# Adjacency masks kept in DRAM as pairs of tiles, and a 14th tile moved per block in the last attention

## The chip, the cores and the metric

The kernel runs on one core of a Trainium2 chip. The metric is the device time of one launch in microseconds (us). A kernel is profiled in one more execution on the chip, and the times quoted from the profile belong to that execution.

## The reference, cut to what matters

The inputs are node features `x` (4096 x 512) and a 0/1 adjacency matrix `adj` (4096 x 4096). Two graph layers with residuals follow each other. All arithmetic is in float32.

```python
# layer 0: adj serves as both patterns, so there is one attention, used twice
h = relu(layernorm(x))
Xw = einsum("hnd,hde->hne", heads(h), W)              # 4 heads of 128
sig = sigmoid(f1[:, :, None] + f2[:, None, :])        # f1, f2: two scores per node and head
att = masked_softmax(adj * sig, adj != 0)
Xn = batchnorm(concat(einsum("hij,hjd->hid", att, Xw)))
emb = batchnorm(elu(Xn @ Wm.T + bm) + Xn)
Y = einsum("hij,hjd->hid", att, heads(emb))           # the same attention again
Y = elu(concat(einsum("hnd,hed->hne", Y, W)))
x = x + batchnorm(elu(Y @ Wd.T + bd) + Y)
# layer 1: another attention over the same adjacency
h = relu(layernorm(x))
feats = einsum("nf,hfo->hno", h, W1)
logits = leaky_relu(e_s[:, :, None] + e_n[:, None, :], 0.2) - 1e10 * (1 - adj)
x = x + relu(concat(einsum("hnm,hmo->hno", softmax(logits), feats) + b))
```

## The kernel before, in words

**Stages.** They follow each other: a front end (layer norm, projection of the nodes, scores); the first attention, called enc; a dense block; the second attention, dec; a second dense block; the values of layer 1; the third attention, gat. `attention` (from L222) is one function that is used three times.

**Blocks and steps.** An attention has eight blocks, one for each of four heads and two halves of the target nodes (2048 of them, `TB`). A block has 32 steps `j`, one for each group of 128 source nodes. In a step, ScalarE computes a tile `e` of 128 x 2048 unnormalized weights (L471 and L472 in enc and dec, L922 in gat), VectorE multiplies it by the mask tile `a` of that step (L473 or L923), and TensorE multiplies it into four PSUM banks (L377). Tiles `e` come from a ring of 8 in enc and 9 in gat (`ebufs` and `EP`).

**Denominators.** Every tile `e` must also be summed over the source nodes. There are three ways to do that. VectorE adds the tile to `acc` (L400 for the first two tiles, L402 after that). TensorE multiplies it by ones (`add_to_den`, L266). Or GpSimd issues two accumulating DMAs, one for each half of the tile, which add it to another tile, `into` (L392). Which steps go where is written in the constants `ENC...` and `GAT...`: the first tuple holds the steps that are moved by DMA, the second those that go to TensorE by ones, and VectorE takes the rest. A third element that is true puts the reading of `into` by TensorE off to step 1 of the next block. In gat `into` is the tile `w` (from block 1 on), and the first move of a block overwrites it. The moves of one half follow each other, since each adds to what the one before it wrote.

**Masks.** The adjacency matrix arrives as float32 and transposed (`adjT`). `copy_adjacency` has GpSimd issue eight DMAs (L502), one after each of the last seven parts of the front end and one more at the end. Each reads 1024 rows by 2048 columns of float32 and writes them as bytes to one DRAM tile of `masks`, of 1024 x 2048, whose rows 128 q to 128 q + 127 are the mask of one step. I call them the casts. The first four hold the masks of the first half of the targets. They are held back until half of `x` is loaded (`half_loaded`).

**Loads.** The SyncE queue loads the mask of each step (L211), 128 rows of 2 KB, to one of five tiles. The load for step `j + 5` waits until VectorE is done with step `j`. The first five are issued in the front end, behind the load of the score row `row0` (L204). The queue also carries the loads of `x` before that (L496). In dec, every fifth step reads the finished tile that enc stored in `ekeep`, and needs no mask. In enc those stores go out on ScalarE's queue in the first two blocks (L362) and on SyncE's later.

**After a block.** The denominators of a block are inverted in the course of the next: they go out to DRAM (L273), come back as columns (L278), are inverted on VectorE (L282, L283), and are spread (L286, L291). GpSimd's queue carries these small DMAs in enc, the same queue as the casts and the accumulating moves; ScalarE's carries them in gat.

Of the kernel before, what the change touches and what calls it, by code (L numbers as in the profile page):

```python
# [31 lines left out]
FP = mybir.dt.float32  # L32
U8 = mybir.dt.uint8
# [6 lines left out]
N, F, H, D, P = 4096, 512, 4, 128, 128  # L40
IB = 512
NIB = N // IB
NJ = N // P
C = IB // P

TB = 2048
NTB = N // TB
SB = TB // IB

MG = 8  # L50
# [13 lines left out]
ENC = (0, 2, 5, 7, 10, 12, 15, 17, 20, 22, 25), (8, 9, 30, 31)  # L64

GAT_FIRST = (0, 2, 4, 6, 8, 10, 12, 14, 16, 18, 20, 22, 24), (30, 31)
GAT = tuple(range(3, 28, 2)), (31,), True

GAT_LAST = (3, 5, 7, 9, 11, 13, 15, 17, 19, 21, 23), (30, 31)

# [15 lines left out]
def kernel(ctx, tc, x, xT, adjT, w0, w0T, v0, wencT, wdecT, vecs, w1, w1T, a1, outT):  # L86
    nc = tc.nc
    consts = ctx.enter_context(tc.tile_pool(name="consts", bufs=1))
# [43 lines left out]


    score = consts.tile([P, 2, NTB, H, NJ // NTB], FP, name="score")
    jcol = consts.tile([P, NTB, H, NJ // NTB], FP, name="jcol")
    jcol2 = consts.tile([P, NTB, H, NJ // NTB], FP, name="jcol2")
    nq = consts.tile([P, NTB, H, NJ // NTB], FP, name="nq")

    def column(t, j, h):
        j = j % (NJ // NTB), j // (NJ // NTB)  # L140
# [20 lines left out]
    ekeep = [[[dram.tile([P, TB], FP, name=f"ekeep{h}_{t}_{k}") for k in range(NJ // KEEP)] for t in range(NTB)]  # L161
             for h in range(H)]

    masks = [[dram.tile([MG * P, TB], U8, name=f"mask{t}_{g}") for g in range(NJ // MG)] for t in range(NTB)]

    def everywhere(d, row, lo, n):

# [36 lines left out]
        return nc.sync.dma_start(rowb, everywhere(d, row, 0, TB))  # L204

    def mask_tile(keep):
        return keep.tile([P, TB], U8, name="a", bufs=5)

    def load_mask(a, tb, j):

        return nc.sync.dma_start(a, masks[tb][j // MG][(j % MG) * P:(j % MG + 1) * P, :])  # L211

    @contextmanager
    def pinned(behind):
# [7 lines left out]
    def attention(what, keep, pools, weights, values, row_of, out, finish, ebufs, modes=None, invert=None,  # L222
# [25 lines left out]
        spool, made, masks0 = pools, 0, list(masks0)  # L248
# [76 lines left out]
        for n, (h, tb) in enumerate(blocks):  # L325
# [4 lines left out]
            into = sums2[0 if n else 1] if moved else None  # L330

            po, ahead, late = [bank() for _ in range(SB - 1)], [], []
            adds, held, stores, at_end, next_row = [], [], [], [], None
            for j in range(NJ):

                with pinned(products_of):
                    for f in later.pop(j, []):
                        f()
                with pinned([a_load, *products_of, last_main] if j else []):
                    if (n, j) in extras:  # L340
                        extras[n, j](a_load)
                    if not last and j == NJ - 10:
                        next_row = next_row_of(*blocks[n + 1])
                e = weight_tile()
                store = j % KEEP == KEEP - 1 and kept is not None
                if store and kept == "read":
                    a_load = nc.sync.dma_start(e, ekeep[h][tb][j // KEEP])
                else:
                    if masks0:
                        a, a_load = masks0.pop(0)  # L350
                    else:
                        a = mask_tile(keep)
                        a_load = load_mask(a, tb, j)

                    with pinned([*(products_of[:1] if kept == "read" and n == 0 and j < 8 else ()),
                                 *(behind if n == 0 and j < EP else ())]):
                        products_of = weights(e, rowb, a, j, h, SB if NJ * n + j < in_parts0 else 1)


                    if stores and (store if n > 1 else j % KEEP == KEEP - 3):  # L360
                        k, t = stores.pop()
                        (nc.sync if n > 1 else nc.scalar).dma_start(ekeep[h][tb][k], t)  # L362
                    if store:
                        stores.append((j // KEEP, e))

                def products():
                    nonlocal last_main, last_ones

                    with tc.issue_after(last_ones.ins) if last_ones is not None else nullcontext():

                        if j == EVICT:
                            po.append(bank())
                            for k, t in ahead:
                                nc.tensor.matmul(po[-1], block(values[h], k), t[:, (SB - 1) * IB:SB * IB],  # L374
                                                 start=(k == 0), stop=False)
                        for s, b in enumerate(po):
                            last_main = nc.tensor.matmul(b, block(values[h], j), e[:, s * IB:(s + 1) * IB],  # L377
                                                         start=(j == 0), stop=(j == NJ - 1))
                    last_ones = None


                if last and invert is not None and j >= NJ - (1 if kept is not None else 4):
                    late.append((j, e))
                else:
                    products()
                if j < EVICT:
                    ahead.append((j, e))
                if invert is not None:
                    if j in moved:

                        for into_half, e_half in in_parts(2, into, e):
                            nc.gpsimd.dma_start(into_half, e_half, **({"accum_op": ALU.add} if j > moved[0] else {}))  # L392
                    elif j in by_ones:
                        held.append(e)
                    else:
                        adds.append(e)
                        if last and kept is not None and j >= NJ - 6:
                            at_end.append(e)
                        elif len(adds) == 2:
                            nc.vector.tensor_add(acc, *adds)  # L400
                        elif len(adds) > 2:
                            nc.vector.tensor_add(acc, acc, e)  # L402

                    if j == NJ - 1:
                        for t in at_end:
                            nc.vector.tensor_add(acc, acc, t)

                    if held and j + 1 not in by_ones:
                        with tc.issue_after(last_main.ins):
                            for t in held:  # L410
                                add_to_den(den, t, not begun)
                                begun = True
                        held = []
                    if j == NJ - 1:
                        with tc.issue_after(last_ones.ins) if last_ones is not None else nullcontext():
                            if moved and not ends_later:
                                add_to_den(den, into, not begun)
                                begun = True
                            add_to_den(den, acc, not begun, not ends_later)
# [58 lines left out]
    with tc.tile_pool(name="keep", bufs=1) as keep:  # L478

        with tc.tile_pool(name="f_small", bufs=1) as small, tc.tile_pool(name="f_work", bufs=2) as work:  # L480
# [18 lines left out]
            def copy_adjacency(n, behind):  # L499

                t, g = divmod(n, NJ // MG)
                cast = nc.gpsimd.dma_start(masks[t][g], adjT[g * MG * P:(g + 1) * MG * P, t * TB:(t + 1) * TB])  # L502
                tc.add_manual_dep(cast.ins, behind.ins.name,
                                  mybir.DependencyInfo(mybir.DependencyClass.Sync, mybir.DependencyReason.DATA),
                                  reason="others first")

            for ib in range(NIB):
# [59 lines left out]
                if ib == SB - 1:  # L567
                    store_rows(rows[0], targets(0))
                    row0 = keep.tile([P, TB], FP, name="rowb", bufs=2)
                    row0_load = load_row(row0, rows[0], 0)  # L570
                    with tc.issue_after(row0_load.ins):
                        masks0 = []
                        for j in range(5):
                            a = mask_tile(keep)
                            masks0.append((a, load_mask(a, 0, j)))
            store_rows(rows[1], targets(1))
# [148 lines left out]
    v1 = xd  # L725

    edge = ctx.enter_context(tc.tile_pool(name="edge", bufs=1))
    with tc.tile_pool(name="l_small", bufs=1) as small, tc.tile_pool(name="l_work", bufs=2) as work:
        x1 = [R[2]] + [small.tile([P, N], FP, name=f"x1_{o}") for o in range(1, C)]

# [215 lines left out]
    with tc.tile_pool(name="gat", bufs=1) as spool:  # L946
# [10 lines left out]

        with tc.issue_after(last_pe.ins):
            attention("gat", spool, spool, gat_weights, v1, lambda h, tb: (rowsg, tb * H + h), out_gat,
                      (scaled_gat, add_to_output), 7, lambda n: (GAT_FIRST, *[GAT] * (H * NTB - 2), GAT_LAST)[n],  # L960
                      (N * TINY, ALU.add), sums=R[2][:, 0:TB], sums2=(row0, R[2][:, TB:N]), row0=row0, in_parts0=3,
                      extras={(0, 1): rest_of_rows, (H * NTB - 1, NJ - 10): load_last, (H * NTB - 1, NJ - 4): add_bias},
                      finish_last=finish_gat)


def _inputs(x, adj, w):
# [5 lines left out]
    return {  # L972
        "x": x,
        "xT": x.T,
        "adjT": adj.T,
        "w0": w["L0_gnn_W"].transpose(1, 0, 2),
        "w0T": w["L0_gnn_W"].transpose(2, 0, 1),
        "v0": w["L0_gnn_V"][..., 0].transpose(2, 0, 1),
# [27 lines left out]
```

## Time and profile before

| what | before |
|---|---|
| median of 3 runs | 3241.08 us (3240.25 to 3242.4) |
| the profiled execution, its time | 3242.24 us |
| its span from first to last instruction | 3240.5 us |
| TensorE matmul, busy | 3187.6 us (98%) |
| VectorE, busy | 2665.8 us (82%) |
| ScalarE, busy | 2581.8 us (80%) |
| bytes moved by DMA | 580.60 MB |
| enc, dec and gat, roughly | 62 to 1040, 1200 to 2065 and 2315 to 3240 us |

Time on the chip around the span is 1.7 us. Matmuls are pipelined, so a busy TensorE isn't TensorE at its peak, and busy shares are averages over stages that have different limits.

### The profile page before, as it was taken

Reading aid. Unit: us, or ns where it says so; the run is one execution under the profiler, and the core shown is the slowest. Engines: PE = TensorE matmul, PEld = TensorE weight load, DVE = VectorE, ACT = ScalarE, POOL = GpSimd, SP = SyncE. Lnnn points to the kernel's source line nnn. Section 1 sums busy time; section 2 is a strip of 40 time slices with the busy share of each in tenths; the row PEclk is TensorE's granted clock in tenths of the full one; section 3 lists DMA queues with packets and bytes.
Section 4 is the critical chain, followed back from the end, with each engine's and each line's share of the span. In section 5 each row is a group of like instructions: output and inputs, shape, how many; then the busy total and the mean of one; then the engine's idle time right before and its main releaser. Section 6 shows DMA issues by size and latency. Waiting matters only on the chain.

```text
span 3240.5 us, 25992 instructions
## 1 busy us (share of the span) xinstructions
PE 3187.6 (98%) x8675; PEld 1477.3 (46%) x8675; DVE 2665.8 (82%) x1945; ACT 2581.8 (80%) x1825; POOL 477.6 (15%) x624
## 2 busy tenths in 40 slices
PE   7999999999999999999999999999999999999998
PEld 6334444444444464444444444448644444444443
DVE  7989999999999665655665665585699999999998
ACT  7999999999997459999999999566765665665663
POOL 3001211211210000000000000025412222122221
PEclk9999999999999999999999999999999999999999
DMA  9998988988986024443443443231489999899996
GB/s 210 198 198 242 273 223 231 268 222 229 268 236 159 7 69 141 143 143 126 139 153 130 133 145 133 62 123 63 130 201 221 214 229 237 218 213 235 229 215 156
DMA packets 212023, 580.60 MB, mean 179 GB/s; under 512 B 25168, under 2 KB 28272, under 8 KB 195888
## 3 DMA queue, kind: packets, MB, share of 16 engines
q0 software_dynamic: 68256, 223.56, 36.5%
q1 hardware_dynamic: 132200, 332.53, 30.1%
q10 hardware_dynamic: 11432, 22.85, 2.0%
q8 instruction: 68, 1.11, 0.1%
q14 instruction: 67, 0.55, 0.0%
HBM read 378.15 MB, written 84.30 MB: 143 GB/s over the span
## 4 chain that ended last, share of the span: by engine, by line
PE 50%; DVE 24%; issue 13%; DMA 9%; ACT 3%; DVEq 0%; POOL 0%; SPq 0%; ACTq 0%; POOLq 0%
PE ps L377 35%; DVE e L923 7%; DVE R L402 7%; PE ps L639 7%; DVE e L473 4%; DMA a<-mask 4%; DMA w<-e 4%; DVE acc L402 4%; PE ps L828 3%; DMA acc<-e 2%; ACT e L471 1%; PE den L266 1%; ACT e L472 1%; PE ps L699 1%; PE ps L374 1%
## 5 line engine op out<-in xcount | busy, mean ns | idle before, releaser
L377 PE MATMUL ps<-e,R 128*128 128x512 f32 x6008 | 2608.1, 595 | 25.0 <-DVE e L473 20.6
L377 PEld LDWEIGHTS ps<-e,R 128*128 128x128 f32 x6008 | 1137.8, 190 | 1489.6 <-issue 1394.3
L473 DVE TENSOR_TENSOR e<-e,a 128x2048 f32<-128x2048 f32 (+1 forms) x470 | 1053.2, 2261 | 388.1 <-ACT e L472 365.0
L471 ACT ACTIVATE e<-rowb,score 128x2048 f32<-128x2048 f32 (+1 forms) x470 | 911.8, 1968 | 78.7 <-PE ps L377 43.4
L472 ACT ACTIVATE e<-e 128x2048 f32<-128x2048 f32 (+1 forms) x470 | 869.3, 1879 | 7.9 <-DVE e L473 2.6
L922 ACT ACTIVATE e<-rowb,nq,jcol 128x2048 f32<-128x2048 f32 x224 | 459.4, 2088 | 265.6 <-DMA w<-e 141.2
L923 DVE SCALAR_TENSOR_TENSOR e<-e,jcol,a 128x2048 f32<-128x2048 f32 (+1 forms) x265 | 591.2, 2260 | 2.8 <-ACT e L922 2.8
L402 DVE TENSOR_TENSOR R<-R,e 128x2048 f32<-128x2048 f32 x128 | 291.1, 2274 | 0.0
L402 DVE TENSOR_TENSOR acc<-acc,e 128x2048 f32<-128x2048 f32 x121 | 276.4, 2285 | 0.9
L392 POOL DMA_DIRECT2D w<-e x178 | 149.4, 845 | 610.8 <-DMA w<-e 294.6
L639 PE MATMUL ps<-R,w 128*128 128x512 f32 x512 | 220.3, 592 | 0.6 <-DVE w L597 0.6
L392 POOL DMA_DIRECT2D acc<-e x146 | 122.5, 888 | 521.0 <-DMA acc<-e 233.4
L291 POOL DMA_DIRECT2D rb<-rinvs x60 | 33.9, 569 | 1054.8 <-DVE R L587 867.2
L639 PEld LDWEIGHTS ps<-R,w 128*128 128x128 f32 x512 | 97.2, 190 | 122.7 <-issue 117.7
L828 PE MATMUL ps<-w1x,hT 128*128 128x260 f32 x512 | 115.5, 384 | 1.4 <-ACT hT L806 1.4
L828 PEld LDWEIGHTS ps<-w1x,hT 128*128 128x128 f32 x512 | 96.5, 190 | 19.8 <-issue 3.3
L922 ACT ACTIVATE e<-w,nq,jcol 128x2048 f32<-128x2048 f32 (+1 forms) x41 | 67.4, 1708 | 25.5 <-DMA R<-e 25.4
L865 POOL TENSOR_TENSOR vacc<-vacc,R 128x128 f32<-128x128 f32 x120 | 65.8, 577 | 45.3 <-ACT R L858 44.9
L662 DVE SCALAR_TENSOR_TENSOR ex<-ex,re 128x512 f32<-128x512 f32 x64 | 44.9, 702 | 32.8 <-ACT re L661 32.6
L660 ACT ACTIVATE ex<-ps,bias 128x512 f32<-128x512 f32 x32 | 22.0, 689 | 58.8 <-PE ps L639 56.4
L858 ACT ACTIVATE R<-ps,rstd 128x128 f32<-128x128 f32 x128 | 38.5, 371 | 29.3 <-PE ps L828 25.6
L266 PE MATMUL den<-e,ones 128*32 128x512 f32 x416 | 51.7, 608 | 3.9 <-DVE e L923 3.9
(175 smaller groups left out, 1255.9 us busy)
## 6 DMA issues: line engine op xcount, KB each, us to landing
a<-mask SPq DMA_DIRECT2D x720, 256.0 KB, 4.1
w<-e POOLq DMA_DIRECT2D x178, 512.0 KB, 6.9
acc<-e POOLq DMA_DIRECT2D x146, 512.0 KB, 6.9
e<-ekeep SPq DMA_DIRECT2D x48, 1024.0 KB, 4.9
ekeep<-e SPq DMA_DIRECT2D x36, 1024.0 KB, 6.9
mask<-in_adjT POOLq DMA_DIRECT2D x8, 2048.0 KB, 105.4
rowb<-rows SPq DMA_DIRECT2D x16, 1024.0 KB, 5.9
rb<-rinvs POOLq DMA_DIRECT2D x60, 256.0 KB, 4.6
```

Of the source, the lines that this page charges most:

```text
L266: last_ones = nc.tensor.matmul(den[s * 32:(s + 1) * 32, :], ones[:, 0:32], t[:, s * IB:(s + 1) * IB], start=start, stop=stop)
L377: last_main = nc.tensor.matmul(b, block(values[h], j), e[:, s * IB:(s + 1) * IB], start=(j == 0), stop=(j == NJ - 1))
L392: nc.gpsimd.dma_start(into_half, e_half, **({"accum_op": ALU.add} if j > moved[0] else {}))
L402: nc.vector.tensor_add(acc, acc, e)
L471: nc.scalar.activation(e, rowb, AF.Tanh, bias=column(score[:, 1], j, h), scale=0.5)
L472: last_act = nc.scalar.activation(e, e, AF.Exp, scale=0.5)
L473: last_dve = nc.vector.tensor_mul(e, e, a)
L639: last = nc.tensor.matmul(z, w[:, fb, o * P:(o + 1) * P], nodes(src[fb], ib), start=(fb == 0), stop=(fb == C - 1))
L828: m = nc.tensor.matmul(banks[k][:, 0:2 * DX], hT[:, fb, c * P:(c + 1) * P], w1x[:, fb, 2 * k:2 * k + 2, :].rearrange("p h x -> p (h x)"), ...
L865: nc.gpsimd.tensor_add(vacc[:, h, :], vacc[:, h, :], block(v1[h], j))
L922: last_act = nc.scalar.activation(e, rowb, AF.Relu, bias=column(nq, j, h), scale=column(jcol, j, h))
L923: last_dve = nc.vector.scalar_tensor_tensor(e, e, column(jcol2, j, h), a, ALU.add, ALU.mult)
```

## The change

**Masks in pairs.** The host orders the adjacency matrix by half of the targets, then by pair of steps, then by the 128 rows, and puts the 2048 columns of the two steps of a pair side by side in a row of 4096. A cast now reads 512 such rows, which follow each other without a gap in DRAM, and writes 512 rows of 4096 bytes, which fill a DRAM tile without a gap as well. The number of casts, their bytes and their place in the program stay. A mask tile holds two steps, there are three of them instead of five, and one DMA of 128 rows of 4 KB loads both steps. The front end loads three pairs ahead. In dec a pair is loaded whole even where one of its steps reads `ekeep`.

**Room.** Three small tiles (`jcol`, `jcol2`, `nq`, 512 bytes a partition each) are taken out of the pool that lives from the start and put into one that is opened after dec.

**Moves in gat.** In blocks 1 to 6 the tiles of 14 steps (3, 5, ..., 29) are moved by DMA instead of 13 (3, 5, ..., 27). In blocks 1, 3 and 5 step 31 still goes to TensorE, so the extra tile is taken from VectorE. In blocks 2, 4 and 6 step 31 goes to VectorE, so in effect the extra tile is taken from TensorE. Blocks 0 and 7 stay.

```diff
-GAT = tuple(range(3, 28, 2)), (31,), True
+GAT = tuple(range(3, 30, 2)), (31,), True
+GAT_EVEN = tuple(range(3, 30, 2)), (), True
...
-    masks = [[dram.tile([MG * P, TB], U8, name=f"mask{t}_{g}") for g in range(NJ // MG)] for t in range(NTB)]
+    masks = [[dram.tile([MG // 2 * P, 2 * TB], U8, name=f"mask{t}_{g}") for g in range(NJ // MG)] for t in range(NTB)]
...
-        return keep.tile([P, TB], U8, name="a", bufs=5)
+        return keep.tile([P, 2, TB], U8, name="a", bufs=3)
...
-        return nc.sync.dma_start(a, masks[tb][j // MG][(j % MG) * P:(j % MG + 1) * P, :])
+        q = j % MG // 2
+        return nc.sync.dma_start(a.rearrange("p k i -> p (k i)"), masks[tb][j // MG][q * P:(q + 1) * P, :])
...
-                    if masks0:
-                        a, a_load = masks0.pop(0)
-                    else:
-                        a = mask_tile(keep)
-                        a_load = load_mask(a, tb, j)
+                    if two_masks is None or j // 2 != two_masks[1]:
+                        if masks0:
+                            both, a_load = masks0.pop(0)
+                        else:
+                            both = mask_tile(keep)
+                            a_load = load_mask(both, tb, j)
+                        two_masks = both, j // 2
+                    a = two_masks[0][:, j % 2, :]
...
-                cast = nc.gpsimd.dma_start(masks[t][g], adjT[g * MG * P:(g + 1) * MG * P, t * TB:(t + 1) * TB])
+                cast = nc.gpsimd.dma_start(masks[t][g], adjT[n * MG // 2 * P:(n + 1) * MG // 2 * P, :])
...
-                        for j in range(5):
+                        for j in range(0, 6, 2):
...
-                      (scaled_gat, add_to_output), 7, lambda n: (GAT_FIRST, *[GAT] * (H * NTB - 2), GAT_LAST)[n],
+                      (scaled_gat, add_to_output), 7, lambda n: (GAT_FIRST, *[GAT, GAT_EVEN] * (H * NTB // 2 - 1), GAT_LAST)[n],
...
-        "adjT": adj.T,
+        "adjT": adj.T.reshape(NJ // 2, 2, P, NTB, TB).transpose(3, 0, 2, 1, 4).reshape(N // 2 * NTB, 2 * TB),
```

More of the change, by code (lines that the diff above doesn't have):

```diff
@@ L134 @@
     score = consts.tile([P, 2, NTB, H, NJ // NTB], FP, name="score")
-    jcol = consts.tile([P, NTB, H, NJ // NTB], FP, name="jcol")
-    jcol2 = consts.tile([P, NTB, H, NJ // NTB], FP, name="jcol2")
-    nq = consts.tile([P, NTB, H, NJ // NTB], FP, name="nq")
     def column(t, j, h):
@@ L332, in attention @@
             po, ahead, late = [bank() for _ in range(SB - 1)], [], []
-            adds, held, stores, at_end, next_row = [], [], [], [], None
+            adds, held, stores, at_end, next_row, two_masks = [], [], [], [], None, None
             for j in range(NJ):
@@ L727 @@
     edge = ctx.enter_context(tc.tile_pool(name="edge", bufs=1))
+    jcol = edge.tile([P, NTB, H, NJ // NTB], FP, name="jcol")
+    jcol2 = edge.tile([P, NTB, H, NJ // NTB], FP, name="jcol2")
+    nq = edge.tile([P, NTB, H, NJ // NTB], FP, name="nq")
     with tc.tile_pool(name="l_small", bufs=1) as small, tc.tile_pool(name="l_work", bufs=2) as work:
```

## The prediction

> **What bounds the kernel now.** I read the windows by stage first. Columns: the stretch and its length, then busy time (and instructions) of PE, PEld, DVE, ACT and POOL, then TensorE's clock, the DMA share and GB/s.
>
> ```profile
> 160.00:200.00 40.00, 37.03 (x115) 14.48 (x113) 35.73 (x18) 38.88 (x22) 0.00 (x0) 1.00 1.05 194
> 600.00:640.00 40.00, 40.00 (x97) 17.78 (x94) 38.70 (x22) 40.00 (x22) 7.51 (x10) 1.00 1.05 276
> 2680.00:2720.00 40.00, 40.00 (x95) 17.76 (x94) 40.00 (x23) 23.48 (x13) 7.72 (x9) 1.00 1.04 245
> ```
>
> In enc's later blocks (second line) ScalarE never stops: 32 x (1.89 + 1.80) = 118.2 us a block, 3.695 us a step. The DMA engines are full from the front end on. In gat (third line) TensorE and VectorE are both never idle, so I looked at which of them sets the end, in the timeline of PE:
>
> ```profile
> 3213.03 1.06 PE L266 MATMUL den<-e,ones 128*32 128x512 f32 x8 [2.33 <-DVE e L923]
> 3217.49 1.93 PE L266 MATMUL den<-e,ones 128*32 128x512 f32 x8 [1.61 <-DVE e L923]
> ```
>
> TensorE waits there 2.33 + 1.61 = 3.94 us for VectorE, so VectorE's sum ends gat, with TensorE 3.94 us behind it.
>
> Then the masks. The waits of VectorE between 100 and 200 us and between 200 and 320 us (total, times, longest):
>
> ```profile
> DVE e L473 <- DMA a<-mask: 7.2, 6, 3.1
> ...
> DVE e L473 <- DMA a<-mask: 5.0, 4, 2.7
> ```
>
> The DMA queues between 24 and 34 us, and between 100 and 200 us (packets, MB, share of 16 engines; q0 is GpSimd's, q1 SyncE's, q10 ScalarE's):
>
> ```profile
> q0 software_dynamic: 434, 0.89, 87.5%
> q1 hardware_dynamic: 323, 0.63, 18.3%
> ...
> q0 software_dynamic: 3582, 7.24, 71.2%
> q1 hardware_dynamic: 3589, 7.32, 21.5%
> q10 hardware_dynamic: 720, 5.24, 12.5%
> ```
>
> q0 is the casts: 0.712 x 1600 / 3582 = 0.318 us for a packet of 2 KB written (8 KB read), one row of 2048 elements. A mask packet takes 0.215 x 1600 / 3589 = 0.096 us. Casts and masks go **one packet for one**: 3582 against 3589. So a mask tile, 128 rows on 16 engines, needs 8 x 0.414 = 3.3 us and more beside a store to `ekeep`, against a demand of 3.695. That is why masks land 15.6 us (median) after issue here and 4.1 over the whole run. Last, in the chain of waits the small DMA behind the casts on GpSimd's queue:
>
> ```profile
> 208.21 35.50 issue
> 243.72 2.47 DMA dcol<-dens
> ```
>
> The casts run from about 24 to 243 us.
>
> **The Trainium skill.** DMA: Bandwidth & Descriptors, "Queues, rings and completion order", says that an engine takes turns between queues a packet at a time. The trace agrees (one for one). In "Why a DMA increments its semaphore by 16 and not by 1" the page says that a descriptor moves one contiguous run of the last dimension, that a contiguous one-dimensional pattern can be split over 16 engines by software, and it names 64 KiB as the longest run. "Rules for kernel authors" says that such a flat transfer becomes few, large descriptors. The trace agrees only that a run makes a packet (cast rows, mask rows); no flat transfer occurs in it.
>
> **The change, part by part.** Sums are made against the profiled execution (span 3240.5, 1.7 us around it, 3242.2, 1.2 above the median).
>
> *Pair loads.* SyncE issues about half as many loads, at 0.32 us each, on a queue that mostly waits for VectorE: nothing. Look-ahead is kept: before, step j + 5 loads after step j; now the pair 2q + 6 loads after step 2q + 1, four steps between them in both, 14.8 us. Packets are 4 KB, 2 x 0.096 = 0.19 us by estimate, still 8 an engine. In dec and gat masks land in some 4 us, so twice the bytes fit the 14.8; dec's unneeded halves add 3 or so tiles of 256 KB a block where DMA is 42% busy. Nothing. Moving `jcol` and the others issues nothing; the shifted addresses could only add waits between stages: 0 to 1 us, I take 0.
>
> *Casts.* This is the part that decides. Source and target have gaps no longer: before, the source's runs were 8 KB within rows of 16 KB; now both sides of a cast are one run. The packet is then not bound to a row. Lower bound: no change or a row of 4096 (16 KB read, 0.64 us). Upper bound: runs of 64 KiB of source, 8 x 0.318 = 2.54 us a packet, 8 packets an engine for a cast, 64 for all. I take the upper bound, since nothing in the pattern any longer names the row. The casts' own time stays, 64 x 2.54 = 163 us, but everything that takes turns with them now waits 2.54 us for each packet:
> - `x`: when casts start (24 us), 308 packets of it are left (0.63 MB at 2 KB), 19.2 an engine. Now 19.2 x (2.54 + 0.09) = 50.5 us instead of 8: the last part of `x` lands at 75, where VectorE began on it at 42.7.
> - The score row behind it: 8 packets an engine, 8 x (2.54 + 0.31) = 23, landing near 98. ScalarE's first step began at about 61.
> - Mask pairs: 8 x (2.54 + 0.19) = 21.8 us each for two steps that take ScalarE 7.4. They land near 120, 142, 164 and 186.
> - The casts end near 24 + 163 + 5 for the packets between them = 192. Until then 4 pairs have come, 8 steps; with the ring of 8 tiles ScalarE can be at about step 14. Before, it was at (192 - 62) / 3.695 = 35. That is 21 x 3.695 = 78 us lost, and no later stage gives it back: ScalarE is enc's bound, TensorE dec's. About 4 of the 5 us that ScalarE idled between 160 and 320 us, behind late masks, come back: **+74 us**, 50 to 95 by how far steps are ahead.
>
> The inverses of block 0, queued behind the casts until 243 so far, are due in block 1, which then begins after the casts have ended: that wait goes, and no new one comes.
>
> *Gat, VectorE.* Blocks 1, 3, 5 lose one add each, 2.20 us from start to start (row L402): 3 x 2.20 = -6.6. Blocks 2, 4, 6 lose none.
>
> *Gat, TensorE.* Blocks 2, 4, 6 lose a group of ones-matmuls: 2546.57 - 2545.69 = 0.88 each, -2.6; with the 3.94 that it needn't wait at the end, -6.6. Both limits agree.
>
> *Gat, DMA.* Six more tiles, 12 transfers of 512 KB on GpSimd's queue (0.85 us each to issue, hidden: GpSimd waits most of the time). What counts is when the last lands, as TensorE reads `into` in step 1. From the timeline, block 3 (last half issued, next read by TensorE):
>
> ```profile
> 2761.42 0.87 POOL L392 DMA_DIRECT2D w<-e  x1 [2.47 <-DMA w<-e]
> ...
> 2776.54 1.06 PE L266 MATMUL den<-w,ones 128*32 128x512 f32 x8
> ```
>
> 15.1 us lie between; a further tile needs about 8.2 (the same half of the tile before was issued at 2753.36) and 6.9 to land, 15.1 in all: no room left. In the six blocks the distance is 12.8, 14.4, 15.1, 16.3, 15.7 and 16.9, so the first two wait 2.3 and 0.7 us, on TensorE, with all its matmuls queued behind. I take 3 in sum, bounds 0 and 9. Gat: -6.6 + 3 = **-3.5**, from -6.6 to +3.
>
> Sum: 3242.2 + 74 - 3.5 = 3312.7; against the median, 3241.1 + 70.5 = **about 3312**.
>
> **Rivals.**
> 1. *Row packets, nothing lost* (the other side of zero). A cast is still cut by row or finer. `x` then needs 19.2 x 0.73 = 14 us, landing at 38, before 42.7; a pair needs 8 x (0.64 + 0.19) = 6.6 us where demand is 7.4: no worse than now. Gat alone: 3237.5. It decides as soon as a packet is short enough that a pair comes in 7.4 us: (7.4 / 8 - 0.19) = 0.73 us, some 18 KB of source. For: a 4096-element row is how both tensors are declared. Against: the packets follow runs, and the rows join.
> 2. *All gains come.* As 1, and the masks catch up (mask packets are half as many, so the 5 us of ScalarE's idling go) and `into` lands in time: 3241.1 - 6.6 - 5 = 3229.5.
> 3. *Half-size packets*, 32 KB: `x` lands at 50, a pair takes 11.7 us; about 10 steps are lost, +33: 3271.
> 4. *The DMA chain becomes gat's bound*: DMA share there is 0.94 to 0.95 a block already, and a tile more is 1/13 of the moves. With row packets and 9 us or more of waits: 3244 to 3250.
>
> **How the numbers follow.** Flat packets 0.60 (own range 3288 to 3335), row packets 0.20 (3234 to 3242), all gains 0.08, half-size 0.07, DMA chain 0.05. The likeliest gives 3312. The range from 3235 to 3332 leaves out 0.08 and a little of rival 1 below, and some 0.07 above. 0.2% is 6.5 us, about what can be told from no change. Faster (below 3234.6): rival 2 and a corner of 1, 0.10. Same (to 3247.6): most of 1, half of 4, 0.21. Slower: 0.69.
>
> **What would show it.** Packets of q0 between 100 and 200 us: some 630 or fewer for flat casts, about 1900 for rows, 3600 for pieces as now. Mask landings of 20 us and more until about 190 us, VectorE waiting on `a<-mask` for tens of us, the first tanh near 100 us. From 320 us on enc and dec run as before. In gat, 178 + 12 = 190 moves into `w`, 3 adds fewer on VectorE, 3 groups of ones-matmuls fewer on TensorE, waits of TensorE on `w<-e` of 0 to 9 us in all, and a smaller wait for VectorE at the end. I am wrong if the casts' packets stay at 16 KB or below, or if engines cut a long packet when another queue asks.

## The result, and the profile after

The changed kernel takes 3331.11 us (median of 4 runs, 3325.54 to 3335.32), beside 3241.71 us for the kernel before in the same session (4 runs). The ratio is 1.0275, with a 95% interval from 1.0263 to 1.0287. The forecast was 3312 us, in a range from 3235 to 3332. So the kernel became slower by about 89 us where 71 were forecast, and the gain expected in gat did not come.

The profiled execution has a span of 3327.4 us, 86.9 more than before. I followed the end of each block in both traces (the start of the ones-matmul that reads `acc`, which is the tile `R` in gat, or of VectorE's last step):

| landmark, us | before | after | difference |
|---|---|---|---|
| first tanh of enc | 59.02 | 141.46 | +82.4 |
| end of enc's block 0 | 199.00 | 292.22 | +93.2 |
| end of enc's block 3 | 561.87 | 647.94 | +86.1 |
| end of enc's block 7 | 1033.40 | 1119.53 | +86.1 |
| end of gat's block 0 | 2433.80 | 2519.94 | +86.1 |
| VectorE's last step of gat | 3215.10 | 3301.29 | +86.2 |

Everything is lost before 300 us. From enc's end to the end of gat's block 0 both kernels take 1400.4 us, and the rest of gat takes 781.30 before and 781.35 after.

The same three stretches of the windows by stage as before, the third moved with its stage:

```profile
160.00:200.00 40.00, 27.36 (x66) 10.83 (x65) 23.45 (x11) 30.64 (x17) 0.00 (x0) 0.85 0.92 156
600.00:640.00 40.00, 38.63 (x90) 16.49 (x90) 39.71 (x22) 40.00 (x23) 5.04 (x6) 1.00 0.85 235
2770.00:2810.00 40.00, 40.00 (x94) 17.67 (x93) 40.00 (x22) 24.78 (x14) 10.14 (x12) 1.00 1.02 258
```

In the first stretch ScalarE now works 30.64 of 40 us instead of 38.88, and VectorE 23.45 instead of 35.73. The other two stretches have the same limits as before. The waits of VectorE from 15 to 320 us (total, times, longest) name what it stood for:

```profile
DVE st L518 <- DMA R<-in_x: 82.8, 2, 66.9
DVE e L475 <- DMA a<-mask: 16.5, 2, 9.3
```

The first line is the front end, waiting for the last parts of `x`. The DMA queues of the changed kernel from 24 to 34 us, and from 100 to 200 us (packets, MB, share of 16 engines):

```profile
q0 software_dynamic: 63, 1.03, 95.7%
q1 hardware_dynamic: 63, 0.12, 3.5%
...
q0 software_dynamic: 612, 8.72, 81.6%
q1 hardware_dynamic: 1172, 4.61, 11.5%
```

In the first pair, a packet of the casts is 1.03 MB / 63 = 16.4 KB written (64 KB read), and takes 0.957 x 160 / 63 = 2.43 us. Sixty-three such packets went with exactly 63 packets of SyncE's queue. Before, the same 10 us had room for 323 packets of that queue, 0.63 MB of `x`. The casts themselves end earlier than before, near 195 us instead of 243, since so little runs beside them.

In gat the page shows the edit: 12 more moves, and 512 KB a mask load.

```profile
a<-mask SPq DMA_DIRECT2D x384, 512.0 KB, 4.3
w<-e POOLq DMA_DIRECT2D x190, 512.0 KB, 7.0
```

TensorE's timeline at the end of gat has the two waits for VectorE that the prediction read before, and they are not smaller:

```profile
3299.23 1.06 PE L265 MATMUL den<-e,ones 128*32 128x512 f32 x8 [2.21 <-DVE e L928]
3303.69 1.94 PE L265 MATMUL den<-e,ones 128*32 128x512 f32 x8 [3.40 <-DVE e L928]
```

They sum to 5.61 us, against 3.94 before: VectorE still ends gat, and by a wider margin.

### The profile page after: what moved, and what is told of

Same layout as the page of the kernel before. It is cut to its first block, busy times and chain, and to the rows that moved or that the text cites. A ratio compares the mean times of both kernels' runs of the same rounds, so it can differ in the third digit from the quotient of the medians.

```text
span 3327.4 us, 25091 instructions
## 1 busy us (share of the span) xinstructions
PE 3187.7 (96%) x8651; PEld 1479.2 (44%) x8651; DVE 2658.9 (80%) x1942; ACT 2581.0 (78%) x1825; POOL 485.7 (15%) x636
## 4 chain that ended last, share of the span: by engine, by line
PE 52%; DVE 21%; DMA 10%; issue 9%; ACT 5%; another core or an unknown queue 2%; POOL 0%; DVEq 0%; SPq 0%; ACTq 0%; POOLq 0%
PE ps L379 38%; PE ps L641 7%; DVE e L928 6%; DMA w<-e 6%; DVE R L404 6%; DVE e L475 5%; PE ps L833 3%; DVE acc L404 3%; ACT e L473 2%; DMA a<-mask 1%; DMA acc<-e 1%; ACT e L474 1%; DMA R<-in_x 1%; PE den L265 1%
## 5 line engine op out<-in xcount | busy, mean ns | idle before, releaser
L394 POOL DMA_DIRECT2D w<-e x190 | 159.8, 848 | 602.6 <-DMA w<-e 317.8
L560 PE MATMUL ps<-w0x,hT 128*128 128x130 f32 x256 | 32.7, 287 | 65.7 <-DVE score L568 64.8
L564 ACT COPY R<-ps 128x256 f32<-128x256 f32 x52 | 19.1, 373 | 73.0 <-PE ps L560 70.9
L518 DVE BATCH_NORM_STATS2 st<-R 128x6 f32<-128x512 f32 x8 | 5.4, 681 | 82.8 <-DMA R<-in_x 82.8
```

## The experiments

The runs ask, in this order: which part of the change costs the time (the first two), whether it is the length of the packets (the next three), which of the starved transfers matters (one), where gat's gain went (two more), and what a version is worth that keeps the good parts (the last). "Gat" in the table is the time from the end of its block 0 to the start of VectorE's last step. It and the end of enc come from one profiled execution of each kernel; a total is the median of 4 to 21 runs, but for the two single ones.

| kernel | masks loaded | moves | longest run of a cast, read | total, us | ratio, 95% interval | enc ends | gat |
|---|---|---|---|---|---|---|---|
| before | single | 13 | 8 KB | 3241.2 to 3241.7 | 1 | 1033.40 | 781.30 |
| changed | pairs | 14 | 64 KB | 3331.11 | 1.0263 to 1.0287 | 1119.53 | 781.35 |
| flat_only | single | 13 | 64 KB | 3338.84 | 1.0289 to 1.0315 | 1129.29 | 781.28 |
| gat_only | single | 14 | 8 KB | 3237.45 | 0.9981 to 0.9994 | 1034.54 | 775.99 |
| cut32 | pairs | 14 | 32 KB | 3296.36 (one run) | | 1084.46 | 783.36 |
| rows16 | pairs | 14 | 16 KB | 3250.06 | 1.0014 to 1.0036 | 1040.96 | 782.23 |
| rows8 | pairs | 14 | 8 KB | 3244.83 | 1.0007 to 1.002 | 1035.97 | 781.85 |
| casts_late | pairs | 14 | 64 KB | 3334.39 (one run) | | 1125.60 | 779.87 |
| pairs8_13 | pairs | 13 | 8 KB | 3243.2 | 0.9997 to 1.0015 | 1033.34 | 781.29 |
| single_gat | pairs, in gat single | 14 | 8 KB | 3238.46 | 0.9984 to 1.0001 | 1034.57 | 776.42 |
| combined | pairs, in gat single | 14 | 8 KB | 3229.56 | 0.9959 to 0.9983 | 1023.78 | 777.48 |

### One part alone: flat casts, and gat's moves

`flat_only` is the kernel before, with only the order of the matrix changed so that a cast's source has no gaps. Single masks and 13 moves stay.

```diff
-cast = nc.gpsimd.dma_start(masks[t][g], adjT[g * MG * P:(g + 1) * MG * P, t * TB:(t + 1) * TB])
+cast = nc.gpsimd.dma_start(masks[t][g], adjT[n * MG * P:(n + 1) * MG * P, :])
...
-        "adjT": adj.T,
+        "adjT": adj.T.reshape(N, NTB, TB).transpose(1, 0, 2).reshape(NTB * N, TB),
```

> The kernel before, with one part of the change alone: the host puts the two halves of the targets one behind the other, so that the source of a cast is one run without gaps, as its target was already. Masks stay single tiles of 128 x 2048 in a ring of five, and gat moves 13 tiles. Theory, the length of the casts' packets: about 64 KB of source in a packet again, some 2.43 us each, the last part of x awaited for 60 to 90 us as in the changed kernel, and a mask load of one step taking 8 x 2.53 = 20 us while casts run, where the changed kernel gets two steps for that: 3330 to 3350 us. Rival, the pairs (three tiles of two steps, 512 KB loads) cost the time: as before, 3241. Rival, the moves in gat cost it: 3241.

It took 3338.84 us, within what the packet-length theory expects. So the gap-free source alone makes the loss, without pairs and without the moves. Gat takes 781.28 us here, as before. It also says something on how `x` comes late. Its DMA queues from 80 to 90 us:

```profile
q0 software_dynamic: 79, 1.03, 95.8%
q1 hardware_dynamic: 70, 0.51, 12.5%
```

The packets of q1 hold 0.51 MB / 70 = 7.3 KB on average. Those of `x` hold 2 KB and those of the score row 8 KB, so most engines were through `x` by then and moved the row behind it. Yet VectorE waited for the last part of `x` until 125.38 us. Here the load landed when the slowest of its engines was done.

`gat_only` is the kernel before with the moves of the change in gat.

```diff
-GAT = tuple(range(3, 28, 2)), (31,), True
+GAT = tuple(range(3, 30, 2)), (31,), True
+GAT_EVEN = tuple(range(3, 30, 2)), (), True
...
-    lambda n: (GAT_FIRST, *[GAT] * (H * NTB - 2), GAT_LAST)[n],
+    lambda n: (GAT_FIRST, *[GAT, GAT_EVEN] * (H * NTB // 2 - 1), GAT_LAST)[n],
```

> The kernel before, with the other part of the change alone: 14 tiles a block moved in gat, in turn from VectorE and TensorE. As predicted: 3.5 us faster, from 6.6 faster to 3 slower. After the changed kernel's trace, in which VectorE waits some 5.6 us for ScalarE within gat, whose tiles are held by moves: 0, within 2 us, and those waits appear here as well. Rival: the waits in the changed kernel came from the larger mask loads, and here the full 6.6 us come.

3237.45 us, 3.85 below the kernel before on the same chip (3241.3). My expectation, made after the trace of the changed kernel had shown no gain in gat, was a gain of at most 2 us and was too small; what came is close to the figure in the prediction, -3.5. In the profile gat itself shortens by 5.3 us. So the moves do gain with single masks, and something in the changed kernel takes that gain away.

### The length of the packets

`rows16`, `rows8` and `cut32` are the changed kernel with a limit on the length of a run in the casts: 16, 8 and 32 KB of source.

```diff
-cast = nc.gpsimd.dma_start(masks[t][g], adjT[n * MG // 2 * P:(n + 1) * MG // 2 * P, :])
+cast = nc.gpsimd.dma_start(masks[t][g], adjT[n * MG // 2 * P:(n + 1) * MG // 2 * P, :],
+                           max_dma_last_dim=16384)
```

> The changed kernel, with the casts' runs capped at 16 KB of source, one row of 4096 elements; everything else as changed. Theory, packet length: packets of 0.6 to 0.65 us, 256 an engine; x lands before 45 us or at most some us late, a mask pair comes in 6.6 us where 7.4 is asked; the time falls to between 3233 and 3245 us. Rival, pairs or gat: it stays near 3331.

> The changed kernel, with the casts' runs capped at 8 KB of source, 2048 elements, the packet of the kernel before. Theory, packet length: packets of 0.32 us; masks, at 4 KB a packet, get twice the bytes for each turn with the casts, a pair in 4 us where 7.4 is asked, so that the 12.2 us of VectorE's waits for masks go and about 5 us of ScalarE's idling with them: 3231 to 3240 us, a few us below the run with 16 KB. Rival, pairs or gat: near 3331.

> The changed kernel with casts cut at 32 KB of source: packets of 1.2 to 1.3 us. By the packet-length theory with some 33 packets of x an engine left when the first cast starts: 33 x 1.35 = 45 us, x lands near 68, the first tanh some 26 us later than before, mask pairs 11.5 us each; 3265 to 3290. The on-record price of half-size packets was 3271. If the loss needs contiguity itself and not length: 3331.

The source stays free of gaps in all three, and the loss falls with the length: 3331.11 at 64 KB, 3296.36 at 32, 3250.06 at 16, 3244.83 at 8. So length matters, not contiguity. The DMA queues from 100 to 200 us, of cut32, rows16 and rows8:

```profile
q0 software_dynamic: 1143, 8.84, 82.7%
q1 hardware_dynamic: 1146, 4.17, 11.1%
```

```profile
q0 software_dynamic: 1876, 7.49, 71.3%
q1 hardware_dynamic: 1826, 7.19, 18.9%
```

```profile
q0 software_dynamic: 3540, 7.15, 70.5%
q1 hardware_dynamic: 2100, 8.21, 21.7%
```

A packet of the casts takes 0.827 x 1600 / 1143 = 1.16 us in the first (some of q0's packets are small ones of other DMAs), 0.61 in the second and 0.32 in the third: in proportion to its bytes. In the first two the packets of the two queues go one for one. In the third SyncE's queue has nothing to send for part of the time, and the masks are no longer late: VectorE has no wait for a mask there at all.

All three were slower than I had expected, rows16 and rows8 by some 5 us and cut32 by 6, beyond the upper ends. The ten runs of rows16 lie further apart than those of any other kernel here, from 3240.34 to 3257.17 us, and cut32 is one run. In cut32 `x` was there at 52 us and not at 68, and the first tanh came 9 us later than before and not 26, so the masks cost more than I had allowed for them. For rows16 and cut32 a part of it is in enc: VectorE waits 11.5 us for masks and 9.2 us for `x` in rows16, and 51.8 and 9.3 in cut32. For rows8 it isn't, as it has neither wait. Two other things are left there. One is gat, below. The other is a wait that takes the place of the one removed, in enc's block 1 (VectorE, 100 to 320 us):

```profile
DVE dcol L281 <- DMA dcol<-dens: 9.5, 1, 9.5
```

Block 0 ended at 194.35 us, 4.65 earlier than before. Its denominators go out on GpSimd's queue behind the casts. They were issued at 200.16, and the DMA that reads them back could be issued only at 244.83, when the casts had ended. VectorE reached the inversion first and waited. Before, it came to that point later and waited 0.59 us. All that block 0 had gained was given back: block 1 ends at 322.44 us, before at 322.07.

### Which starved transfer matters

`casts_late` is the changed kernel, with flat casts, but the first of them is held until all of `x` is loaded and not half of it.

```diff
-                if ib == NIB // 2 - 1:
-                    half_loaded = load
+                half_loaded = load
```

> The changed kernel, its casts still flat, but the first casts held until all of x is loaded (before: half of it). x then lands by 45 and the front end runs as before. If the long packets hurt whatever is behind them (theory): the score row needs 8 turns, first tanh near 70, mask pairs 20 to 22 us each until the casts end near 205 to 215, VectorE waits 60 us or more on masks, total 3295 to 3325. If the late x was the loss by itself: 3245 to 3265.

3334.39 us. `x` comes in time now and the wait for it is gone, but nothing is gained: the total lies within the runs of the changed kernel, and block 0 of enc ends at 292.30 us, where it ended at 292.22. My theory had the right sign, and its range of 3295 to 3325 was still too low. ScalarE's first step, and VectorE's multiplications by masks in this kernel:

```profile
80.59 0.72 ACT L473 ACTIVATE e<-rowb,score 128x512 f32<-128x512 f32 x1 [21.32 <-DMA rowb<-rows]
```

```profile
122.04 4.49 DVE L475 TENSOR_TENSOR e<-e,a 128x2048 f32<-128x2048 f32 x2 [12.16 <-DMA a<-mask]
142.67 4.49 DVE L475 TENSOR_TENSOR e<-e,a 128x2048 f32<-128x2048 f32 x2 [11.61 <-DMA a<-mask]
165.27 4.49 DVE L475 TENSOR_TENSOR e<-e,a 128x2048 f32<-128x2048 f32 x2 [15.90 <-DMA a<-mask]
186.55 4.49 DVE L475 TENSOR_TENSOR e<-e,a 128x2048 f32<-128x2048 f32 x2 [14.46 <-DMA a<-mask]
```

The score row was issued at 53.96 us, and took until 80.59, 26.6 us. A pair of masks arrives every 20.6 to 22.6 us. These are the steps of the prediction without the late `x` in front of them. The waits for masks are 76.1 us in sum, where the changed kernel has 16.5 for masks and 82.8 for `x`. In both VectorE comes to step 10 only when the casts are over (at 203.88 here, 205.20 there). As long as casts run, SyncE's queue gets one packet for each of theirs, whether these packets hold `x` or masks.

That the two ends come so close is in part chance. In the changed kernel GpSimd had issued five of the eight casts when the front end stood still for `x`. They were done at 127 us, and for 3 us no cast moved. In that gap most of the first three pairs of masks came through at once, as the queues from 127 to 130 us show; casts_late has no such gap.

```profile
q1 hardware_dynamic: 281, 1.00, 81.9%
q0 software_dynamic: 1, 0.00, 0.0%
```

### Where gat's gain went

`pairs8_13` is rows8 with the 13 moves of before in gat. `single_gat` is rows8 with single mask loads in gat, out of the same pairs in DRAM.

```diff
-                    if two_masks is None or j // 2 != two_masks[1]:
+                    if kept is None:
+                        a = keep.tile([P, TB], U8, name="a", bufs=5)
+                        q = j % MG // 2
+                        a_load = nc.sync.dma_start(
+                            a, masks[tb][j // MG][q * P:(q + 1) * P, j % 2 * TB:(j % 2 + 1) * TB])
+                    elif two_masks is None or j // 2 != two_masks[1]:
...
-                    a = two_masks[0][:, j % 2, :]
+                    if kept is not None:
+                        a = two_masks[0][:, j % 2, :]
```

> Pairs with casts cut at 8 KB of source and the 13 moves of before. So far: 8 KB pieces with 14 moves stand at +3.5 us, the 14 moves alone at -3.9, and in the profiles gat (from the end of its block 0 to VectorE's last step) changed by -5.3 with single loads and by +0.5 with pair loads. Theory A (a pair load of 512 KB only hurts where the chain of accumulating moves has no room): with 13 moves gat is as before, the total 3241 to 3245, near 8 KB pieces with 14 moves. Theory B (the pair loads cost gat some 4 us whatever is moved): 3246 to 3251. In both, enc ends 1 to 3 us later than before, as the first block's denominators wait behind the casts.

> As the changed kernel with casts cut at 8 KB, but gat loads each step's mask by itself, 128 rows of 2 KB (256 KB) in five tiles, out of the same pairs in DRAM. If the pair load takes gat's gain: gat shortens by 4 to 5 us as it did with single masks, the total is 3238 to 3241, and VectorE's waits for ScalarE in gat fall from some 5 us to under 3. If the loss has another cause (addresses, stage order): 3243 to 3247 as with pair loads.

3243.2 and 3238.46 us, as theory A and the first of the two alternatives have it; only that enc ends later didn't come in pairs8_13 (1033.34 us, before 1033.40). With the kernel before and gat_only the four corners are there. Gat takes 781.28 and 781.30 us with single loads and 13 moves, 775.99 and 776.42 with single loads and 14, 781.29 with pairs and 13, and 779.87 to 783.36 with pairs and 14 (changed, cut32, rows16, rows8, casts_late; 781.7 on average). Pair loads cost nothing with 13 moves, and with 14 they cost the gain. The size of the load and the ring (three tiles of two steps, or five of one) change together here; no run parts them. VectorE's waits for ScalarE from 2420 to 3330 us (total, times, longest), of the changed kernel, rows8, gat_only and single_gat:

```profile
DVE e L928 <- ACT e L927: 5.2, 5, 3.0
```

```profile
DVE e L929 <- ACT e L928: 4.4, 3, 2.9
```

```profile
DVE e L924 <- ACT e L923: 0.6, 1, 0.6
```

```profile
DVE e L935 <- ACT e L934: 0.8, 2, 0.6
```

In the kernel before and in pairs8_13 there is no such wait. The longest one in the changed kernel, in the timelines of ScalarE and of VectorE:

```profile
2862.63 4.08 ACT L927 ACTIVATE e<-rowb,nq,jcol 128x2048 f32<-128x2048 f32 x2 [3.58 <-DMA w<-e]
```

```profile
2864.75 2.35 DVE L928 SCALAR_TENSOR_TENSOR e<-e,jcol,a 128x2048 f32<-128x2048 f32 x1 [3.04 <-ACT e L927]
```

ScalarE stood 3.58 us for a tile of the ring that a move had not released yet, and VectorE waited 3.04 us for ScalarE's tile. This is the chain of moves, and where it bites: four of the five waits, 4.8 of the 5.2 us, begin with ScalarE standing for a move (the fifth with a small DMA of the denominators). How a load of 512 KB delays a move more than two of 256 KB is not seen directly. The median move takes 6.7 to 7.0 us from issue to landing, with either load. The slowest, over 550 us of the middle blocks, takes 12.2 to 13.3 us with pairs (changed, rows8, pairs8_13) and 10.7 to 11.0 with single loads (before, gat_only, single_gat). That agrees with bursts of packets in front of single moves, but I made no run that shows it.

### A version that beats both

`combined` is single_gat, with one edit more: in enc the denominators of block 0 are inverted three steps later, and the spreads of the second half of them come four steps after the first, not seven, so that they still fit the block.

```diff
-                j = INVERT + slack + (7 if hop is nc.gpsimd else 11) + s % 2 + s // 2 * (7 if hop is nc.gpsimd else 5)
+                j = INVERT + slack + (7 if hop is nc.gpsimd else 11) + s % 2 + s // 2 * ((4 if slack else 7) if hop is nc.gpsimd else 5)
...
-                   4 if kept == "write" and n == 0 else 0)
+                   7 if kept == "write" and n == 0 else 0)
```

> Pairs in enc and dec with casts cut at 8 KB, single mask loads and 14 moves in gat (as in the run before), and for the first block of enc the inversion of the denominators three steps later (its spreads closer together), so that VectorE doesn't stand behind the small DMA that is queued after the casts. In the run before enc's first block ended 6.0 us earlier than in the kernel before, and VectorE's wait of 10.3 us for that DMA gave it all back (enc's end +1.2). If that wait is what gives it back: the wait goes to under 2 us, enc ends 3 to 6 us earlier than before, total 3231 to 3235. If the masks or ScalarE set block 1 anyway: 3237 to 3240, as the run before.

3229.56 us (6 runs), a ratio of 0.9971 with an interval from 0.9959 to 0.9983: 12 us faster than the kernel before, and a little more than I had expected. The runs lie between 3228.36 and 3236.81 us. VectorE's waits from 100 to 320 us are down to one kind:

```profile
DVE e L481 <- ACT e L480: 6.1, 6, 2.8
```

The wait for `dcol` is gone, and so are those for masks. Enc ends 9.6 us earlier than before, gat is 3.8 us shorter. Pairs of masks, then, were worth something in enc, as long as the casts came in short packets: block 0 ends 4.6 to 6.0 us earlier than before in the four kernels with pairs and pieces of 8 KB. I made no run with the later inversion and single masks; in the kernel before, the wait that it removes is 0.59 us.

## Why the prediction was right, and where it wasn't

The direction and the cause, long packets taking turns with short ones, were right. The size was less so: the median lies 0.9 us below the upper end of the range, and two of the four runs lie above it. The profiled execution takes 3329.2 us, 16.5 more than the sum of 3312.7. Of these, 12.1 are in the term for enc and 3.5 in the one for gat.

**Packets of 64 KB, one for one: right.** The upper of the two bounds held. No trace of the kernel before showed a packet of that length, so it was a choice by argument. The packet was estimated at 2.54 us, and takes 2.43. It is the point that decided the sign, and rivals 1 and 2 with their short packets fell with it.

**`x` lands at 75: wrong, it was 125.** Two things were off. The first is how much was left. SyncE's queue up to 24 us, in the changed kernel and before:

```profile
q1 hardware_dynamic: 3725, 7.32, 84.3%
...
q1 hardware_dynamic: 3944, 7.75, 87.9%
```

`x` has 8.39 MB, so 1.07 MB were left and not 0.63: 522 packets of 2 KB, 33 an engine and not 19.2. At 2.52 us a turn that alone leads to 106 us. Why less had gone by then stays open. The casts are not the reason, as casts_late had moved 7.35 MB by then, and its casts begin only after 30 us. The second is that the step divided by 16 engines, which stand unevenly, as flat_only shows: to last until 125 us, the slowest engine must have had some 40 packets to go. But casts_late shows that this miss was not what made the total too low: with `x` in time the masks take the loss over.

**The score row in 23 us and pairs each 21.8 us: right in size.** casts_late has 26.6 us for the row, and 20.6 to 22.6 for the pairs. In the changed kernel itself the row came behind the late `x`, so the times of day were other than predicted (the first tanh at 141 us, not near 100), and so was the name on the wait. The test that I had set, VectorE waiting tens of us for masks, would have failed, although the mechanism held.

**Casts end near 192: right,** 195 us, in part by luck. Their 64 packets an engine take 64 x 2.43 = 156 us and not 163; 3 us without casts, and some 12 for the packets between them where 5 were allowed, make up for it.

**21 steps of ScalarE lost, +74: the term that was mis-sized, +86.** For block 0 the loss was put at 78 us and is 93.2. What was done when the casts ended was nearly as predicted: VectorE had multiplied 8 steps at 192 us, as forecast, and ScalarE had begun 12 tiles at 195 and stood 7.4 us for the next, whose place in the ring was still being stored, where the prediction has step 14. That the 8 agree is luck, as the prediction has the pairs one after another from 98 us on and the trace has three of them at once near 130. But ScalarE was not what the rest of the block waited for. Its tiles ahead still had to be multiplied by masks, and VectorE came to step 10 only at 205.20. VectorE's timeline there and after the block's last multiplication, and the window from 210 to 230 us:

```profile
205.20 4.49 DVE L475 TENSOR_TENSOR e<-e,a 128x2048 f32<-128x2048 f32 x2
...
289.88 2.48 DVE L585 COPY R<-ps 128x512 f32<-128x512 f32 x4
```

```profile
210.00:230.00 20.00, 20.00 (x59) 8.25 (x58) 19.93 (x10) 19.97 (x12) 0.00 (x0) 1.00 0.47 175
```

ScalarE and TensorE are busy as well, but from 200 to 293 us ScalarE waits 5.4 us and TensorE 0.7 us for VectorE, and VectorE for nobody. From 205.20 to 289.88 it needs 84.7 us for 22 steps (and two multiplications of the next block), 3.85 a step. With this figure in place of ScalarE's lead, the prediction's own 8 steps at 192 us lead to 192 + 24 x 3.85 = 284.4, 85 us later than before. Of the other 8 us of block 0, some 5.5 went by as the masks of steps 8 and 9 came only at 196.26, so that step 10 began at 205.20 and not near 200, and 2.3 lie between the last multiplication and the end of the block. The prediction had the 8 steps in hand, then took ScalarE's lead as work done. Half-size packets (rival 3) were priced by the same step at 3271, and measured 3296.36, although `x` and the pairs came nearly as that rival says.

**What comes back later: 4 us predicted, 7.1 measured.** Block 1, which has no casts beside it any more, gives back 4.1, as predicted. Blocks 2 and 3 give back 3.0 more; they had no casts before either, and why stays open.

**The inverses of block 0: right.** In the changed kernel no wait for `dcol` appears, as the casts end before block 0 does. I had not looked at that wait for the rivals with short packets, where it turned out to be the one that takes the place of the wait removed (9.5 us in rows8).

**Pair loads and room at nothing: right up to gat, wrong there.** Enc's end to the end of gat's block 0, with dec's unneeded halves and the moved small tiles, takes 1400.4 us in both. In gat, with 14 moves, it was 5 us. The loads there had been judged by their own landing, which stays in time. What they do to the moves was left out.

**Gat, -3.5: nearly that for the moves alone (-3.85 in gat_only), and 0 in the changed kernel.** That the first came so near is in part luck. The DMA chain's cost, 3 us, was placed on TensorE, as it reads `into`. TensorE has no such wait in gat_only, where gat shortens by 5.3 us, and one of 0.5 us in the changed kernel. With pair loads it came by another way, from a move to a tile of the ring, to ScalarE, and to VectorE, whose 5.2 us of waits take most of what 6.6 us of adds had freed. Rival 4 named the chain, with waits of 9 us or more; it holds for the place, not for the price.

The Trainium skill, DMA: Bandwidth & Descriptors, "Queues, rings and completion order", also says that a turn holds typically 9 to 17 descriptors. No run here shows turns of that kind: if descriptors were gathered in a packet for SyncE's queue, its single rows of 2 KB would not alternate one for one with pieces of 64 KB. What a profile counts as a packet is what took turns here.

## What to carry to other kernels

Closing the gaps of a DRAM-to-DRAM DMA can lengthen its packets, as it did for the casts here from 8 to 64 KB, and the loads beside it then waited for that length at each of their own packets; where a small transfer with a deadline runs beside a large one, cut the large one short. Price a starved stage by the engine that consumes the late data, not by the engine that can run ahead of it, and a load by its slowest DMA engine, not by the mean over 16. After removing a wait, look at what is queued behind the same transfers elsewhere: the gain of pairs in enc was there, and was given back at the next small DMA until that was moved too.

## What the runs showed of the hardware

- Casts between DRAM tensors ran in pieces of 64 KB of source with nearly the same time for each KB as pieces of 8 KB: 2.43 us and 0.32 us, 0.038 and 0.040 a KB. Longer pieces made the casts hardly faster in themselves; they ended earlier (195 us, not 243) because they kept others out.
- Turns stay one packet for one even when one is 64 KB and the other 2 KB (63 against 63 in 10 us), so while both queues had something to send, the length of their packets set their shares.
- DMA engines can be far apart on the same queue: in flat_only most had moved on to the score row by 80 to 90 us while one or more still had `x` to bring until 125. Why they stand so unevenly stays open.
- Changing one mask load of 256 KB a step into one of 512 KB for two steps moved nothing in gat with 13 moves a block (781.29 us, and 781.30 before), and cost some 5 us with 14 (781.7 on average, and 776.0 to 776.4 with single loads).
